# Expert blocks of a hybrid convolution/attention kernel: the first layer's products regrouped from pairs to triples

## The chip, the cores and the metric

The kernel runs on one core of one Trainium2 chip, in fp32 throughout. The metric is the time of one execution in device microseconds, as the median of repeated runs. The engines named below are TensorE (PE, its weight loads PEld), VectorE (DVE), ScalarE (ACT), GpSimd (POOL) and the DMA-issuing SyncE (SP).

## The reference, cut to what matters

The program computes a grid layer with sampled attention, a window attention and, last, a mixture of four experts over 4096 tokens of 384 channels. The change touches the experts:

```python
scores = jnp.einsum('bsd,de->bse', x, gate_w) + gate_b       # 4 experts
probs = jax.nn.softmax(scores, axis=-1)                      # the two best are kept and normalised
h = jax.nn.gelu(jnp.einsum('bsd,edh->ebsh', x, w1) + b1[:, None, None, :], approximate=False)
y = jnp.einsum('ebsh,ehd->ebsd', h, w2) + b2[:, None, None, :]
out = jnp.einsum('bse,ebsd->bsd', masked, y)                 # x: 384 channels, h: 1536, y: 384
```

Each token goes through two of the four experts. For one expert, the first layer is a product of the tokens (384 channels) with a 384 x 1536 matrix, followed by a bias and a GELU; the second layer is a product with a 1536 x 384 matrix.

## The kernel before, in words

The first 1690 us or so of the execution are the grid layer, the window attention and the router; they were placed by a planner and by the framework's scheduler. The change touches them at two places: the number of buffers of the `kv` tile in `keys` (line 2356), and the loop in `outputs` (line 2447) that hands POOL one weight sum per token tile for the first expert block.

The experts are 25 blocks in a fixed order (`ORDER`, line 43): blocks 0 to 12 hold 512 rows, 13 to 15 hold 256, 16 to 24 hold 128. Blocks 1, 2 and 12 follow a 512-row block directly; 3, 5, 7, 9, 10 and 11 stand behind a 128-row block, 4, 6 and 8 behind a 256-row one. Inside this stage the instructions of all five engines stand in the order in which the program writes them (a manual schedule), and every engine works its queue in order.

A block takes its rows by an indirect DMA a block ahead (`gather`), its weights by SP (`first_weights`, `second_weights`), turns the rows on PE into channels on partitions (`turn`: four transposes into a PSUM tile and one copy to `xT`, for each of three channel groups), and then runs the two layers.

For 512 and 256 rows (`long_block`) the first layer saves multiplications. The hidden units come in 12 groups of 128, taken as six pairs; the tokens come in two halves of `m` = 256 (or 128) columns. Channel groups 0 and 1, two hidden groups and two token halves form a 2 x 2 by 2 x 2 block product that is done with seven products P1 to P7 (a Winograd form) in place of eight; channel group 2 is multiplied plainly (`plain`). The class `Pair` holds the steps: `alpha` (P1, P5 and a copy of P1 by ACT), `beta` (P2, P3), `gamma` (P6, accumulated over P1 in the left half of the PSUM tile `y`), `after_gamma` (a second copy, then two DVE additions), `delta`, `after_delta`, `epsilon`, and `gelu`. The sums of weights that the products need are made by POOL (`first_sums_steps`: four additions per half of the weights, so eight per block), the sums of token halves by DVE (`token_sums`: four additions).

The second layer is always the seven-product form (`second_product`, six products of 192 columns for each token tile), with weight sums on POOL (`second_sums`) and sums of the hidden values on DVE (`hidden_sums`). `add_rows`, `add_bias` and `store_rows` add the weighted results to the output rows that `rows_so_far` has read, and POOL stores them by indirect DMA. A block of 128 rows (`short_block`) uses plain products in both layers.

While block j runs, its `hooks("start")` puts on POOL's queue the second half of its own weight sums, the second layer's sums, the reading of the output rows, and the first half of the next block's weight sums; `hooks("between")` issues the weights and the gather for block j + 2. The next block's rows are turned, and its token sums made, inside the second layer of the present one.

PSUM tiles come from three pools: `ltr` (2 buffers, transposes), `lmm` (4 buffers: the pairs' `x` and `y`, and some accumulators) and `lph` (2 buffers). SBUF scratch of the first layer is `snap` and `third`, two buffers each.

## Time and profile before

| what | us |
|---|---|
| median of 15 runs | 2721.13 (2711.2 to 2728.9) |
| the profiled execution's own time | 2719.35 |
| its span in the trace | 2717.7 |
| PE busy | 2517.0 (93%) |
| DVE busy | 1801.6 (66%) |
| POOL busy | 1357.3 (50%) |
| ACT busy | 1102.8 (41%) |
| PE busy in the stretch 1800 to 2000 us (experts) | 197.93 of 200 |
| ACT, DVE, POOL busy in that stretch | 47.90, 89.28, 90.18 |

The experts' stage runs from about 1691 us (the first transposes of block 0) to the end. One line of the profile stands for one instruction or for a run of equal ones; an fp32 product of PE is two instructions, so "x2" in a line of PE is one product. A line gives the start, the duration, the engine, the line of the kernel, the operation, the tile written and those read, their shapes, and in brackets how long the engine had been idle and what ended that.

### The profile page before, as it was taken

What the parts mean: (1) busy time and instruction counts of PE and PEld (TensorE: products, weight loads), DVE (VectorE), ACT (ScalarE), POOL (GpSimd) and SP (SyncE); (2) the same over time, 40 slices, a digit from 0 to 9 for tenths busy, and PEclk for the clock granted to TensorE, in tenths of its full rate; (3) what the DMA queues carried; (4) which work ended last, traced back from release to release, by engine and by line L of the source; (5) the groups of instructions that cost most, each with busy time, mean ns of one, the idle gap of its engine ahead of it and who ended that gap; (6) DMA issues with size and microseconds to landing.
All of it is one profiled execution on the core that took longest, in us unless ns stands there. A gap on an engine that the chain in (4) does not pass through costs nothing. (4 is left out here: it accounts for less than half of the span.)

```text
span 2717.7 us, 39372 instructions
## 1 busy us (share of the span) xinstructions
PE 2517.0 (93%) x15017; PEld 1590.4 (59%) x15017; DVE 1801.6 (66%) x2921; ACT 1102.8 (41%) x1818; POOL 1357.3 (50%) x1132
## 2 busy tenths in 40 slices
PE   8877976899999999999999997899999999999999
PEld 5434533333333333333366664788878888888888
DVE  3655856998999999999957666644354454434443
ACT  5543542565666666666533331222232222122222
POOL 1334845665566556666401255444384454544453
PEclk9877977999999999999999998899999999999999
DMA  7554437555555665555221313235455545544441
GB/s 212 150 142 133 127 103 208 168 161 173 146 156 169 192 177 165 161 153 160 81 93 47 120 59 104 87 121 170 150 190 184 179 146 183 184 164 158 164 144 36
DMA packets 263321, 395.44 MB, mean 146 GB/s; under 512 B 134674, under 2 KB 207634, under 8 KB 262748
## 3 DMA queue, kind: packets, MB, share of 16 engines
q1 hardware_dynamic: 214912, 230.43, 27.5%
q0 software_dynamic: 47504, 162.42, 19.5%
q8 instruction: 119, 1.95, 0.3%
q14 instruction: 70, 0.57, 0.1%
q10 hardware_dynamic: 716, 0.07, 0.0%
HBM read 335.95 MB, written 70.06 MB: 149 GB/s over the span
## 5 line engine op out<-in xcount | busy, mean ns | idle before, releaser
L1443 PE MATMUL ps<-q,k 64*64 64x512 f32 (+1 forms) x1632 | 380.4, 583 | 33.5 <-DVE S L1475 16.9
L1448 PE MATMUL ps<-t,o 64*64 64x512 f32 (+3 forms) x1536 | 351.8, 572 | 0.0
L1324 POOL DMA_INDIRECT win<-table,widx x192 | 283.5, 1477 | 69.5 <-issue 24.7
L1015 POOL DMA_INDIRECT ga<-img,pidx x168 | 192.0, 1143 | 234.1 <-DVE w L972 70.1
L2564 POOL DMA_INDIRECT out<-rows,ei x67 | 67.3, 1004 | 415.2 <-DVE rows L2557 394.0
L1475 DVE SCALAR_TENSOR_TENSOR S<-t,bw,ps 128x1024 f32<-128x1024 f32 x192 | 237.1, 1277 | 32.0 <-PE ps L1448 29.5
L1385 ACT ACTIVATE t<-win,bw 128x1056 f32<-128x1056 f32 x192 | 207.4, 1092 | 120.0 <-DVE S L1475 99.4
L1443 PEld LDWEIGHTS ps<-q,k 64*64 64x64 f32 x1632 | 103.9, 134 | 251.8 <-issue 187.0
L1548 POOL TENSOR_TENSOR S<-S,pbs 128x896 f32<-128x896 f32 (+1 forms) x69 | 136.7, 1982 | 203.2 <-DVE t L1396 197.5
L1553 ACT ACTIVATE S<-S 128x2048 f32<-128x2048 f32 x96 | 183.4, 1911 | 96.9 <-DVE S L1540 88.8
L1567 PE MATMUL po<-S,v 128*64 128x512 f32 x768 | 191.5, 610 | 24.0 <-ACT S L1553 23.5
L1396 DVE SCALAR_TENSOR_TENSOR t<-win,bw,t 128x1056 f32<-128x1056 f32 (+3 forms) x169 | 196.1, 1196 | 12.6 <-ACT t L1385 12.5
L2661 PE MATMUL b<-w,h 128*128 128x192 f32 x1044 | 180.3, 326 | 0.0
L856 PE MATMUL pcv<-qpad,wc 64*64 64x256 f32 x1728 | 144.0, 414 | 34.7 <-issue 32.5
L2661 PEld LDWEIGHTS b<-w,h 128*128 128x128 f32 x1044 | 171.3, 190 | 2.4
L1540 DVE TENSOR_TENSOR S<-S,pbs 128x2048 f32<-128x2048 f32 (+1 forms) x96 | 158.9, 1657 | 12.4 <-ACT pbs L1529 12.4
L2493 DVE COPY d_xT<-e_tr 128x512 f32<-128x512 f32 (+2 forms) x75 | 37.6, 511 | 172.4 <-PE e_tr L2490 152.3
L2600 ACT COPY snap<-y 128x256 f32<-128x256 f32 (+1 forms) x96 | 33.8, 352 | 271.0 <-PE y L2583 263.2
L2257 POOL DMA_INDIRECT tab_d<-ent,si x64 | 65.9, 1030 | 146.2 <-DVE selw L2250 126.4
L2615 DVE TENSOR_TENSOR snap<-y,snap 128x256 f32<-128x256 f32 (+1 forms) x96 | 38.3, 399 | 151.1 <-ACT snap L2614 136.7
L2757 ACT ACTIVATE h<-ph,b1c 128x128 f32<-128x128 f32 x108 | 30.8, 368 | 265.1 <-PE ph L2751 265.1
L856 PEld LDWEIGHTS pcv<-qpad,wc 64*64 64x64 f32 x1728 | 83.4, 145 | 89.1 <-issue 69.7
(413 smaller groups left out, 5745.3 us busy)
## 6 DMA issues: line engine op xcount, KB each, us to landing
w<-in_L_ffn_w SPq DMA_DIRECT2D x50, 2304.0 KB
img<-in_x SPq DMA_DIRECT2D x48, 256.0 KB
q<-q_d SPq DMA_DIRECT2D x48, 256.0 KB
x<-in_x SPq DMA_DIRECT2D x8, 768.0 KB
q_d<-qt SPq DMA_DIRECT2D x24, 256.0 KB
v_d<-qkvw SPq DMA_DIRECT2D x32, 192.0 KB
k<-k_d SPq DMA_DIRECT2D x48, 128.0 KB
v<-v_d SPq DMA_DIRECT2D x24, 256.0 KB
```

What stands on the lines that cost most here:

```text
L856: nc.tensor.matmul(ps[s][h * GC : (h + 1) * GC, :], wc[half, t, c, :], qpad[half, c, y0 : y0 + 8, dx : dx + WI], start=(t == 0), stop=(t = ...
L1015: nc.gpsimd.indirect_dma_start(out=ga[:, g].rearrange("p s c -> p (s c)"), out_offset=None, in_=img[b][:, :], in_offset=bass.IndirectOffse ...
L1324: i_ = nc.gpsimd.indirect_dma_start(out=win[:, : (WROWS - free_rows(nb)) * WIN], out_offset=None, in_=tables[h // 2][:, :], in_offset=bass ...
L1385: i_ = nc.scalar.activation(t.rearrange("p y x -> p (y x)"), wins[p, e][:, :n], AF.Copy, scale=weight(p, e, 0),)
L1396: state["gate"] = nc.vector.scalar_tensor_tensor(tf, wins.pop((p, e))[:, WIN : WIN + ts[p, e].shape[1] * WIN], weight(p, e, 1), tf, ALU.mu ...
L1443: made.append(nc.tensor.matmul(ps[HALF[1 - r], e, q_at], k[HALF[r], 2 * kp + e, :], q[HALF[r], q_at], start=(step == 0), stop=(step == 1 a ...
L1448: made.append(nc.tensor.matmul(ps[HALF[r], d, at], os_[p, d][HALF[r], :], wholes[p, d][HALF[r], at.start // WI : at.stop // WI, 0:WI], sta ...
L1475: nc.vector.scalar_tensor_tensor(st[:, e, :].rearrange("p (y x) -> p y x", x=WI), wholes.pop((p, e))[:, :, 1:WIN], weight(p, e, 3), ps[:, ...
L1540: state["gate"] = nc.vector.tensor_tensor(at_, at_, bc(pbss[p // KP][:, cols_], 1, 2), ALU.add)
L1553: nc.scalar.activation(Ss[p], Ss[p], AF.Exp)
L1567: nc.tensor.matmul(pos[i][0][HALF[f], :], vs[i][:, 2 * kp + e, :], Ss[p][:, e, FULL[f]], start=(first and e == 0), stop=(last and e == 1),)
L2661: nc.tensor.matmul(out[:, k * NH : (k + 1) * NH], h[:, v, k * P : (k + 1) * P], w[:, v, :], start=(start and v == 0 and k == 0), stop=True ...
```

## The change

Blocks of 512 rows get another first layer; blocks of 256 rows keep the pairs (now in a function `by_pairs`, with the same steps); blocks of 128 rows keep plain products. For 512 rows the hidden groups are taken as four triples, and all three channel groups, three hidden groups and two token halves form a 3 x 3 by 3 x 2 block product that is done with 15 products q1 to q15 in place of 18. The class `Trio` holds its steps. Six products (`alpha(0)` to `alpha(5)`) accumulate one after the other in the right half of the PSUM tile `x`, and ACT copies the running sum to SBUF after each of the first five; five products (`beta(0)` to `beta(4)`) accumulate in the right half of the PSUM tile `y`, and DVE adds the running sum to a copy after each. `shared`, `one`, `two` and `three` are the other four products.

`by_threes` interleaves the first five alphas of the next group with the present group's other products by a written string of letters: `A` is an alpha of the group ahead, `a5` the present group's sixth alpha, `b` a beta of the present group, `q`, `r`, `s` and `p` are `shared`, `two`, `three` and `one`, `w` a beta of the group before, `v`, `z` and `u` GELUs, `f` a product of the second layer that fills the last group. The first five alphas of a block's first group are issued by `begin` inside the block before.

POOL now makes 13 weight sums of 256 columns per half of the weights (26 per block), DVE 12 sums of token halves in two parts and ACT one negated copy; the copies of the transposes to `xT` move from DVE to ACT; the transposes and the token sums stand at earlier places in the second layer of the block before; P1 and P2 of the second layer are split to wait for the last GELUs. In the router stage, POOL is handed up to four sums per token tile, and `kv` has two buffers in place of three. The scratch `xc` has one buffer of ten parts in place of two of three; `th`, `tg` and `tc` have two each.

```diff
-                kv = c2.tile([P, 2 * NC], F32, tag="kv", bufs=3, name=f"kv{b}_{k}")
+                kv = c2.tile([P, 2 * NC], F32, tag="kv", bufs=2, name=f"kv{b}_{k}")
...
-                i_ = next(sums, None)
-                if i_ is not None:
+                for i_ in itertools.islice(sums, 4):
                     then(i_, y_)
...
+        t = flat.rearrange("p (k g j) -> p k g j", k=6, j=P)
+        n0, n1, n2, n3, n4, n5 = (t[:, k] for k in range(6))
+        d["A", half] = dict(
+            q1=a31, q2=a11, q3=n5, q4=n2, q5=a12, q6=n3, q7=n4, q8=a13, q9=n1, q10=n0, q11=a21, q12=a23, q13=a22,
+            q14=a32, q15=a33,
+        )
+        for out_, one, other, op in (
+            (n0, a21, a33, ALU.add), (a31, a31, a32, ALU.add), (n1, a21, a31, ALU.add), (a31, a11, a31, ALU.add),
+            (n2, a32, a31, ALU.subtract), (n2, n2, a33, ALU.subtract), (n3, a13, a23, ALU.subtract),
+            (n4, a21, n3, ALU.subtract), (n3, n3, a22, ALU.add), (n5, a31, a12, ALU.add), (n5, n5, n3, ALU.subtract),
+            (a23, a23, a33, ALU.add), (a23, a23, a22, ALU.subtract),
+        ):
+            yield nc.gpsimd.tensor_tensor(out_, one, other, op)
...
-            nc.vector.tensor_copy(d["xT"][:, c, :n], pt[:, :n])
+            nc.scalar.copy(d["xT"][:, c, :n], pt[:, :n])
...
+            if part == 0:
+                nc.scalar.mul(x9, b11, -1.0)
+            for out_, one, other, op in (
+                (
+                    (x0_, b12, b11, ALU.subtract), (b12, b12, b22, ALU.subtract), (x1, b12, b32, ALU.subtract),
+                    (x2, b11, x1, ALU.subtract), (x3, b11, b22, ALU.subtract),
+                ),
+                (
+                    (x6, b32, b31, ALU.subtract), (x7, x6, b12, ALU.subtract), (x5, b21, b31, ALU.add),
+                    (x4, b21, b22, ALU.subtract), (b21, b11, b21, ALU.subtract), (x8, b22, b31, ALU.add),
+                    (b32, b22, b32, ALU.add),
+                ),
+            )[part]:
+                nc.vector.tensor_tensor(out_, one, other, op)
...
+        class Trio:
...
+            def alpha(self, k):
+                if k == 0:
+                    self.x = lmm.tile([P, 512], F32, tag="mm", name="x")
+                    self.th = dh.tile([P, 512], F32, tag="th", bufs=2, name="th")
+                    self.tg = dh.tile([P, 512], F32, tag="tg", bufs=2, name="tg")
+                    self.tc = dh.tile([P, 256], F32, tag="tc", bufs=2, name="tc")
+                self.product(("q10", "q11", "q9", "q1", "q2", "q4")[k], self.x, self.right, start=k == 0)
+                if k < 5:
+                    to = (
+                        self.th[:, self.right], self.th[:, self.left], self.tc[:, : self.m], self.tg[:, self.left],
+                        self.tg[:, self.right],
+                    )[k]
+                    nc.scalar.copy(to, self.x[:, self.right])
+
+            def beta(self, k):
+                if k == 0:
+                    self.y = lmm.tile([P, 512], F32, tag="mm", name="y")
+                self.product(("q15", "q12", "q6", "q8", "q7")[k], self.y, self.right, start=k == 0)
+                if k < 4:
+                    to = (
+                        self.tc[:, : self.m], self.th[:, self.left], self.tg[:, self.left], self.tg[:, self.right]
+                    )[k]
+                    nc.vector.tensor_tensor(to, self.y[:, self.right], to, ALU.add)
+                else:
+                    nc.vector.tensor_tensor(self.y[:, self.both], self.y[:, self.both], self.th[:, self.both], ALU.add)
+
+            def shared(self):
+                self.z = lph.tile([P, 512], F32, tag="ph", name="z")
+                self.product("q3", self.z, self.left, start=True)
+                to = self.tg[:, self.right]
+                nc.vector.tensor_tensor(to, self.z[:, self.left], to, ALU.add)
+
+            def one(self):
+                self.product("q5", self.z, self.left)
+                to = self.tg[:, self.left]
+                nc.vector.tensor_tensor(to, self.z[:, self.left], to, ALU.add)
+
+            def two(self):
+                self.product("q13", self.y, self.left)
+
+            def three(self):
+                self.product("q14", self.x, self.left)
+                to = self.x[:, self.left]
+                nc.vector.tensor_tensor(to, to, self.tc[:, : self.m], ALU.add)
...
+        def begin(d):
+
+            if d is None or short(d) or middle(d):
+                return
+            d["first"] = t = Trio(d, 0)
+            for k in range(5):
+                t.alpha(k)
+                yield
...
+            for g in range(last + 1):
+                was, t, ahead = t, ahead, Trio(d, g + 1) if g < last else None
...
+                for what in (
+                    "A0 v a5 w4 A1 z q b0 A2 r b1 A3 s b2 A4 u p b3" if g < last else
+                    "f v a5 w4 f z q b0 f r b1 f s b2 f u p b3 f f f b4 x"
+                ).split():
...
+                    elif what == "q":
+                        t.shared()
+                    elif what == "r":
+                        t.two()
+                    elif what == "s":
+                        t.three()
+                    elif what == "p":
+                        t.one()
...
+                    elif was and what[0] == "w":
+                        was.beta(k)
...
+            if nxt:
+                token_sums(nxt, 0)
             second_product(d, "P7", b1_, range(HV), False)
...
+            third, more = second_steps(d, "P3", b3_, range(HV), False), begin(nxt)
+            for _ in third:
+                next(third, None)
+                next(more, None)
+            for _ in more:
+                pass
...
+            if nxt:
+                token_sums(nxt, 1)
             add_rows(d, low, 1, b3_)
             store_rows(d, low)
```

## The prediction

> **What bounds the kernel now.** The page's slices come first: in the experts' stage (from 1691 us) PE stands at 9 nearly throughout. Then one 512-row block, cut at its last first-layer products, in the table by stretches.
>
> ```profile
> PE   8877976899999999999999997899999999999999
> ```
>
> ```profile
> core 0: us, PE busy (x) PEld busy (x) DVE busy (x) ACT busy (x) POOL busy (x), PEclk, DMA share, GB/s
> 1771.40:1800.10 28.70, 28.55 (x124) 22.70 (x123) 9.65 (x19) 13.30 (x28) 25.85 (x21) 1.00 0.44 143
> 1800.10:1828.90 28.80, 28.80 (x181) 28.56 (x180) 17.54 (x30) 1.53 (x3) 1.48 (x2) 1.00 0.26 93
> ```
>
> PE is filled in both layers at granted clock 1.00; DVE and ACT have room, POOL is full in the first half and idle in the second. So PE's products, and waits that interrupt them, set the time. The groups by shape give the prices of the steps between products.
>
> ```profile
> L2616 DVE TENSOR_TENSOR x<-x,snap 128x512 f32<-128x512 f32 x78 | 54.6, 700 | 8.3 <-DVE snap L2615 0.5
> L2615 DVE TENSOR_TENSOR snap<-y,snap 128x256 f32<-128x256 f32 x78 | 33.1, 424 | 134.4 <-ACT snap L2614 120.0 <-issue 14.3
> L2600 ACT COPY snap<-y 128x256 f32<-128x256 f32 x78 | 29.0, 372 | 242.8 <-PE y L2583 237.7 <-remote 3.9 <-ACT third L2631 1.0
> L2122 POOL TENSOR_TENSOR wa<-w 128x384 f32<-128x384 f32 x30 | 30.5, 1015 | 2.5 <-PE y L2590 2.2
> L2523 POOL TENSOR_TENSOR wb<-w 128x1152 f32<-128x1152 f32 x15 | 39.4, 2627 | 0.0
> ```
>
> Last, the timeline of the one place in a 512-row block where PE waits today, for the delays between engines.
>
> ```profile
> 1773.99 0.59 PE L2583 MATMUL y<-xc,wa 128*128 128x256 f32 x2
> ...
> 1774.63 0.37 ACT L2614 COPY snap<-y 128x256 f32<-128x256 f32 x1 [0.86 <-issue]
> ...
> 1774.86 0.59 PE L2583 MATMUL x<-d_xT,wa 128*128 128x256 f32 x2
> ...
> 1775.03 0.42 DVE L2615 TENSOR_TENSOR snap<-y,snap 128x256 f32<-128x256 f32 x1 [2.68 <-ACT snap L2614]
> 1775.56 0.70 DVE L2616 TENSOR_TENSOR x<-x,snap 128x512 f32<-128x512 f32 x1
> 1775.57 0.30 PEld L2583 LDWEIGHTS y<-d_xT,w 128*128 128x128 f32 x2 [0.52 <-issue]
> 1775.60 0.67 PE L2583 MATMUL y<-d_xT,w 128*128 128x256 f32 x2
> ...
> 1776.11 0.59 PE L2590 MATMUL y<-d_xT,w 128*128 128x256 f32 x2
> ...
> 1776.34 0.69 ACT L2620 ACTIVATE h<-x,b1c 128x512 f32<-128x512 f32 x1 [1.34 <-DVE x L2616]
> ```
>
> The reader is to see: products follow each other by 0.431 us. A reader of PSUM starts 0.63 after its product's start (1773.99, 1774.63). The stalled product counts as begun at 1775.68 (the next comes 0.43 later), so 0.23 after the DVE addition's end (1775.45); after an ACT copy the weight load follows by 0.05, hence 0.16. ACT starts 0.08 after a DVE addition (1776.26, 1776.34). And P7, which writes the left half of `y`, waits for L2615, which reads the right half: a PSUM tile is waited for whole.
>
> **Products (a gain).** A pair has nine products of 256 columns and one of 512: 6 x 11 = 66 steps of 0.431. The triples have 4 x 15 = 60. 6 x 0.431 = 2.59 us saved per block. The stall shown (1775.68 for 1775.29: 0.39) goes too. Together -2.98.
>
> **Wait 1: `th` (the chain is not three apart here).** alpha(0) of the group ahead is copied into `th`, which has two buffers; that buffer is the one of the group before, and is free only when beta(4)'s 512-column addition has read it. The built instruction order lists this wait on ACT's copy, in the second and third triple of each block. But beta(4) (`w4`) is issued after A0, one product before A1, which needs the copy. From the start of w4: addition from 0.63 to 1.33, copy from 1.41 to 1.78, A1 at 1.94 in place of 0.43: 1.51 lost. Behind the waiting copy stand two GELUs (0.69 each, needed a group later) and A1's copy; the second GELU ends 0.2 before A2's copy is due, so nothing more is lost. 2 x 1.51 = 3.02 per block.
>
> **Wait 2: `two`.** q13 goes to the left of `y`, whose right half the addition of beta(0) is reading; the built order shows the wait, as for P7 above. From b0: the addition runs 0.63 to 1.05, r counts at 1.28; its place is 0.86. 0.42, in four groups (0.52 in the last, where a 0.326 us filler stands for an alpha): 1.78 per block. The other betas are three products apart, 1.29 against 1.28: covered, by nothing to spare; in the last group 1.19, 0.09 late three times: 0.27.
>
> **Starting a block.** An alpha with its copy turns round in 0.63 + 0.37 + 0.16 = 1.16. Between two second-layer products (0.65) it comes every 1.08: four times 0.08, and 0.30 at A1, where only a5 lies between: 0.62.
>
> Sum per 512-row block: -2.98 + 3.02 + 1.78 + 0.27 + 0.62 = **+2.71**. For the 12 blocks after block 0: +32.5. Block 0 alone has its five alphas bare (4 x 0.73), before its gain; the start before had stalls of its own (1.2 to 3 us in PE's waits); I take 0, between -3 and +8.
>
> **Weight and token sums (POOL, DVE).** A 256-column addition is estimated at 0.75 on the line through 1.015 and 2.627, with the 0.05 between dependent ones about 0.79: 13 take 10.3 where four took 4.3. Between 512-row blocks POOL's idle second half holds them. Behind a 128-row block there is no such room:
>
> ```profile
> 1887.54 0.98 POOL L2564 DMA_INDIRECT out<-rows,ei  x1 [0.31 <-issue]
> 1894.87 0.99 POOL L2536 DMA_INDIRECT rows<-out,ei  x1 [6.34 <-DMA out<-rows,ei]
> ```
>
> ```profile
> 1898.28 1.10 DVE L2505 TENSOR_TENSOR xc<-d_xT,xc 128x256 f32<-128x256 f32 x1
> ```
>
> POOL waits for a store to land, then reads rows and sums from R = 1894.87. The token addition that takes 0.42 elsewhere takes 1.10 beside POOL's sums: DVE lets POOL's addition end first. In the changed order, DVE's bias addition waits for the rows (1902.55 before, R + 7.7), 0.6, then come the seven sums of part 1, five beside POOL at 0.8 each until R + 12, two more at full speed, a row addition (0.6), the addition of `shared` and that of b0, done at R + 14.5, so r counts at R + 14.7. PE reaches the block 2.5 later than before (five alphas and their stalls; 1902.45 + 2.5 = R + 10.1), A0, a5, A1 (0.30 late), q, b0, A2 take it to R + 13.0, and wait 2 would let r go at R + 13.2: **1.5 late**, between 0 (DVE not slowed) and 3.5 (three more waits of 0.7). Six such blocks: 9.0. Block 11 has four gathers ahead of its second half's sums, not one (3 x 1.27): 1.5, between 0 and 4. Behind the three 256-row blocks only three alphas have products between them (two bare, 0.65 more each), and the first waits about 1 for token sums; those blocks' own 2 us wait (P6 on DVE's rows, below) shrinks: +2 each, between -1 and +4: 6.
>
> ```profile
> PE b L2661 <- DVE rows L2557: 5.4, 3, 2.1
> ```
>
> **Elsewhere.** The 26 early sums end before POOL's next work (idle 31 us until 1639.62); two `kv` buffers suffice, since PE issues the product that frees one before the matmuls that refill it. Bounds 0 to +5 (the wait of PE's `pa` for `kv` is 3.3 in all). ACT gains three copies of about 0.6 and one negation per block where it is idle (1.53 busy of 28.8): hidden; without cover, 0.6 each.
>
> **Clock.** The 2.06 us wait above is followed by a granted clock of 0.59 over 2002 to 2006; waits of 1.23 and 1.27 near 1711 and 1715 are not, nor is one of 1.7 between 2260 and 2400 (1.00 over 2200 to 2400). At 1.51 I take 0, up to +10.
>
> The Trainium skill's "TensorE: Matmul & The Clock Gate", section "Why this matters for your kernels", asks only for no idle gap over some 3 us. By it not even the 2.06 us gap would have mattered, and the term and its upper bound would be 0; here the row decides.
>
> **Sum.** 32.5 + 0 + 9.0 + 1.5 + 6 = 49.0 on the profiled execution's own 2719.35: 2768. That execution lies 1.8 below the median of 15, so 2770.
>
> **Rivals.**
> Late sums hidden: DVE and POOL lose nothing behind short blocks, only the waits inside the block stay: 2721 + 33 = 2754. With 0.16 instead of 0.23 for DVE's way back to PE (the copy's; six times 0.07 in each of 13 blocks, 5 in all) and the low bounds of start and 256-row blocks, 2743. For it: DVE was idle 10 us before those sums. Against: 1.10 for 0.42.
> Sums and clock at their upper bounds: 49 + 6 x 2 + 2.5 + 3 x 2 = 69.5, so 2790, and up to 2813 with clock, start and `kv`; half-way in, 2783 on. For it: 2002 to 2006.
> The other side: the two waits overlap work. If DVE served beta(4) and beta(0) so that waits 1 and 2 together cost under 2.1 of their 4.8 per block, the blocks would gain; with both at 0, 12 x -2.1 = -25, and -8 with the sums: 2696 to 2713. The waits stand in the built order, so only the prices could be wrong, by half.
> The announced spacing is itself a rival that fails: were all links three apart, wait 1 would be 0.
>
> **How the numbers follow.** Likeliest, 0.52: 2758 to 2783. Late sums hidden 0.22, upper bounds 0.19, other side 0.05, no change 0.02. Leaving out the far ends of the rivals gives 2745 to 2798. Within 0.2% (5 us, what can be told from no change): 0.02; faster 0.05; slower 0.93.
>
> **What would show it.** In the changed profile: twice per 512-row block a PE gap near 1.5 us at A1, released by an ACT copy to `th` that itself waited for a 512-column DVE addition; a gap of 0.4 before q13 in each triple, released by DVE; 512-row blocks 2.7 us longer, 57.5 to 60.2; gaps of 1 to 2 us in the first triple behind 128-row blocks. I am wrong if PE runs A0, a5, w4, A1 at 0.43 steps.

## The result and the profile after

The changed kernel takes 2768.02 us (median of 9 runs, 2753.8 to 2778.51) where the kernel before takes 2721.86 (46 runs): 1.0166 times as long, 95% interval 1.0150 to 1.0182. The forecast was 2770. The profiled execution took 2764.45 with a span of 2762.7, 45.0 more than the span before. So the total agrees; the terms it was made of agree less well, and this is the more useful reading.

PE's waits in the experts, longest in total first (total, times, longest), from the waits of the changed kernel from 1690 us on:

```profile
PE x L2694 <- ACT th L2711: 38.4, 27, 6.4
PE y L2694 <- DVE tc L2721: 12.1, 19, 2.1
...
PE y L2631 <- DVE snap L2663: 2.7, 5, 1.3
...
PE x L2694 <- POOL wa L2150: 1.8, 1, 1.8
```

The first line is wait 1 of the prediction (A1's product waits for ACT's copy to `th`), 24 of 27 in pairs in the blocks behind block 0. The second is wait 2 (q13 waits for DVE's addition of the first beta) and, in its longest cases, the late token sums. The waits of P6 for DVE's rows, 5.4 us before, don't occur in this profile (in a second profile of the changed kernel they are 2.6), and for POOL's first-layer sums there is one wait of any size, in block 11.

Wait 1 and wait 2 in block 1, on the timelines of PE, DVE and ACT (start, duration, what; in brackets the idle time and its end):

```profile
1789.01 0.59 PE L2694 MATMUL x<-xc,wa 128*128 128x256 f32 x2
1789.44 0.59 PE L2694 MATMUL x<-d_xT,wa 128*128 128x256 f32 x2
1789.87 0.59 PE L2694 MATMUL y<-d_xT,wa 128*128 128x256 f32 x2
1791.72 0.70 PE L2694 MATMUL x<-xc,w 128*128 128x256 f32 x2 [1.25 <-ACT th L2711]
1792.26 0.59 PE L2694 MATMUL z<-d_xT,wa 128*128 128x256 f32 x2
1792.69 0.59 PE L2694 MATMUL y<-xc,w 128*128 128x256 f32 x2
1793.12 0.59 PE L2694 MATMUL x<-xc,wa 128*128 128x256 f32 x2
1793.80 0.70 PE L2694 MATMUL y<-xc,w 128*128 128x256 f32 x2
1794.34 0.59 PE L2694 MATMUL y<-d_xT,w 128*128 128x256 f32 x2
```

```profile
1790.51 0.70 DVE L2723 TENSOR_TENSOR y<-y,th 128x512 f32<-128x512 f32 x1 [0.87 <-PE y L2694]
...
1793.32 0.42 DVE L2721 TENSOR_TENSOR tc<-y,tc 128x256 f32<-128x256 f32 x1
```

```profile
1791.29 0.37 ACT L2711 COPY th<-x 128x256 f32<-128x256 f32 x1 [1.99 <-DVE y L2723]
```

These are A0, a5, w4 at steps of 0.43, then A1 at 1.85 behind w4, where 0.43 would do: w4's product, DVE's addition of 512 columns (ends 1791.21), ACT's copy (1791.29 to 1791.66), A1 at 1791.72. The product behind A1 comes at 0.54, not 0.43. So the wait costs 1.42 + 0.11 = 1.53; the prediction had 1.51. q13 at 1793.80 comes 0.68 behind A2, with 0.54 behind it: 0.25 + 0.11 = 0.36, where the prediction had 0.42. The addition that it waits for ends at 1793.74.

Behind a 128-row block (block 3), DVE, PE and POOL:

```profile
1916.30 0.84 DVE L2597 SCALAR_TENSOR_TENSOR rows<-b2r,en,rows 128x384 f32<-128x384 f32 x1 [4.84 <-DMA rows<-out,ei]
1917.07 0.95 DVE L2556 TENSOR_TENSOR xc<-d_xT 128x256 f32<-128x256 f32 x1
1918.05 0.83 DVE L2556 TENSOR_TENSOR xc<-xc,d_xT 128x256 f32<-128x256 f32 x1
...
1921.40 0.41 DVE L2556 TENSOR_TENSOR xc<-d_xT 128x256 f32<-128x256 f32 x1
...
1922.93 0.41 DVE L2721 TENSOR_TENSOR tc<-y,tc 128x256 f32<-128x256 f32 x1
```

```profile
1920.70 0.59 PE L2694 MATMUL x<-xc,wa 128*128 128x256 f32 x2
1923.40 0.70 PE L2694 MATMUL y<-xc,w 128*128 128x256 f32 x2 [2.10 <-DVE tc L2721]
```

```profile
1909.23 0.99 POOL L2584 DMA_INDIRECT rows<-out,ei  x1 [7.55 <-DMA out<-rows,ei]
```

With R = 1909.23 the rows let DVE go at R + 7.1 (forecast R + 7.7), the additions take 0.83 to 0.95 beside POOL's sums and 0.41 when those are done, b0's addition ends at R + 14.1 and q13 starts at R + 14.2 (forecast R + 14.7).

What each stretch of the experts takes, from the first transposes of a block to those of the block behind it (differences of starts on PE's timeline; "+" joins blocks):

| stretch | before | changed | difference |
|---|---|---|---|
| block 0 | 67.21 | 69.13 | +1.9 |
| block 1; block 2 | 57.47; 57.46 | 59.87; 59.87 | +2.4 each |
| 16+3, 18+5, 20+7, 22+9, 23+10 | 73.58, 73.58, 73.58, 73.78, 73.58 | 78.08, 77.81, 77.26, 76.56, 77.75 | +4.5, +4.2, +3.7, +2.8, +4.2 |
| 24+11 | 73.57 | 79.66 | +6.1 |
| 17+13+4, 19+14+6, 21+15+8 | 110.31, 108.30, 108.36 | 110.23, 109.99, 110.84 | -0.1, +1.7, +2.5 |
| block 12 to the end | 75.69 | 81.98 | +6.3 |

In a 512-row block the changed kernel transposes the next rows 12 second-layer products, 3.9 us, earlier (behind P4, not behind P6): so block 0 is really 5.8 longer and block 12 is 2.4 longer. The start of the stage lies 2.5 later than before. These differences add up to the 45.0.

### The profile page after: what moved, and what is told of

Read it like the earlier page. It is cut to its first block, busy times and chain, and to the rows that moved or that the text cites. A ratio compares the mean times of both kernels' runs of the same rounds, so it can differ in the third digit from the quotient of the medians.

```text
span 2762.7 us, 39983 instructions
## 1 busy us (share of the span) xinstructions
PE 2504.6 (91%) x15017; PEld 1574.3 (57%) x15017; DVE 1884.9 (68%) x3132; ACT 1141.4 (41%) x1932; POOL 1525.5 (55%) x1366
## 5 line engine op out<-in xcount | busy, mean ns | idle before, releaser
L2783 PE MATMUL b<-w,h 128*128 128x192 f32 x1044 | 188.7, 326 | 0.0
L857 PE MATMUL pcv<-qpad,wc 64*64 64x256 f32 x1728 | 136.5, 409 | 36.7 <-issue 34.8
L2605 DVE SCALAR_TENSOR_TENSOR rows<-b,en,rows 128x192 f32<-128x192 f32 x232 | 85.3, 411 | 121.0 <-PE b L2783 95.6
L2694 PE MATMUL x<-xc,w 128*128 128x256 f32 x312 | 101.2, 406 | 42.3 <-ACT th L2711 38.4
L2517 ACT COPY d_xT<-e_tr 128x512 f32<-128x512 f32 (+2 forms) x75 | 32.8, 453 | 220.0 <-PE e_tr L2514 220.0
L2150 POOL TENSOR_TENSOR wa<-w 128x256 f32<-128x256 f32 x130 | 109.4, 842 | 16.5 <-PE y L2694 12.4
```

The source lines that it names most:

```text
L857: nc.tensor.matmul(ps[s][h * GC : (h + 1) * GC, :], wc[half, t, c, :], qpad[half, c, y0 : y0 + 8, dx : dx + WI], start=(t == 0), stop=(t = ...
L2783: nc.tensor.matmul(out[:, k * NH : (k + 1) * NH], h[:, v, k * P : (k + 1) * P], w[:, v, :], start=(start and v == 0 and k == 0), stop=True ...
```

## The experiments

The runs fell on chips of two kinds. On those with the numbers 14, 1 and 10 the kernel before takes 2634 to 2636 us, on number 11 it takes 2723. For the first profiles of both kernels no number is on record; by their time (2722) they belong with number 11. Where an expectation speaks of the second or the other chip, the kind is meant. The experts' blocks take the same time on both kinds (999.9 and 999.8 us in the last column for the changed kernel), block 0 excepted. Every ratio is against the kernel before, run beside it. The last column is the time from block 1's first transposes to the end, in one profile; the kernel before has 959.3 and 957.5 in two profiles, and 3.9 has to be added to these for a comparison, because its transposes stand 3.9 later. The rows with "+" build on "all three", each on the one with "+" above it; a later place for the gather replaces the earlier one.

| kernel | median | before | ratio (95%) | blocks 1 to 12 and their short ones |
|---|---|---|---|---|
| changed | 2768.02 | 2721.86 | 1.0166 (1.0150 to 1.0182) | 999.9 |
| changed, faster kind of chip | 2677.36 | 2633.71 | 1.0168 (1.0151 to 1.0185) | 999.8 |
| third `th` | 2636.34 | 2636.06 | 1.0002 (0.9990 to 1.0013) | 964.9 |
| q13 by b0 | 2657.27 | 2636.06 | 1.0082 (1.0065 to 1.0099) | 985.7 |
| bias later | 2669.51 | 2636.06 | 1.0123 (1.0104 to 1.0141) | 995.7 |
| all three | 2615.07 | 2636.06 | 0.9919 (0.9902 to 0.9936) | 943.3 |
| + late gather | 2617.67 | 2633.71 | 0.9938 (0.9921 to 0.9954) | 947.5 |
| + wider start | 2611.97 | 2633.71 | 0.9925 (0.9909 to 0.9942) | 944.2 |
| copies on DVE | 2681.01 | 2633.71 | 1.0178 (1.0161 to 1.0195) | 1007.4 |
| + gather behind all sums | 2703.90 | 2722.65 | 0.9935 (0.9913 to 0.9957) | 944.4 |
| + rows first | 2700.10 | 2722.65 | 0.9921 (0.9891 to 0.9951) | 941.8 |
| + early gather | 2602.15 | 2635.67 | 0.9877 (0.9854 to 0.9899) | 930.5 |

**Wait 1 taken away.**

```diff
-                    self.th = dh.tile([P, 512], F32, tag="th", bufs=2, name="th")
+                    self.th = dh.tile([P, 512], F32, tag="th", bufs=3, name="th")
```

> The changed kernel with three buffers for th in place of two, nothing else. Theory (wait 1 of the prediction): in the changed profile A1 starts 1.85 us after the product before it, where 0.43 would do, and the product after it follows at 0.54 where 0.43 would do, so the wait costs 1.53; it stands twice in each of 13 blocks, 40 us. With a third buffer the copy of group g+1 has nothing to wait for: 2768 - 40 = 2728 us, between 2722 and 2736, and the waits of x for th fall from 38.4 us to under 8 (block 0 has one of 6.4 that DVE's own standstill makes). Rival: the waits only show that DVE and ACT set the pace, and the time comes back at the next link of a chain (q13 or a beta waiting for DVE): 2755 to 2768, with the waits of y for tc risen from 12 us to 30 or more.

The changed kernel's 1.0168 on a kernel before of 2636.06 is 2680; this one has 2636.34, 44 less. Blocks 1 and 2 take 56.81 and 56.82, 3.06 and 3.05 less than 59.87, two waits of 1.53. PE's waits:

```profile
PE y L2694 <- DVE tc L2721: 14.2, 21, 2.8
...
PE x L2694 <- ACT th L2711: 1.0, 2, 0.6
```

The time did not come back at q13: the first line was 12.1 and is 14.2. The rival, that DVE and ACT set the pace, falls. One buffer of 2 KB a partition is the whole difference between a loss of 1.7% and none.

**Wait 2 taken away.**

```diff
                 self.product(("q15", "q12", "q6", "q8", "q7")[k], self.y, self.right, start=k == 0)
+                if k == 0:
+                    self.product("q13", self.y, self.left)
...
-                    "A0 v a5 w4 A1 z q b0 A2 r b1 A3 s b2 A4 u p b3" if g < last else
-                    "f v a5 w4 f z q b0 f r b1 f s b2 f u p b3 f f f b4 x"
+                    "A0 v a5 w4 A1 z b0 A2 q b1 A3 s b2 A4 u p b3" if g < last else
+                    "f v a5 w4 f z b0 f q b1 f s b2 f u p b3 f f f b4 x"
```

> The changed kernel with q13 issued directly after the first beta's product and ahead of DVE's addition to it, and the string otherwise the same with q moved to where r stood; th keeps two buffers. Theory (wait 2): q13 starts 0.25 late in three groups of a block and 0.36 in the last, each with 0.11 more at the product after it, 1.55 us per block; all go, and the next beta stands three products behind: 13 x 1.55 = 20, so 2748 us, between 2742 and 2756; wait 1 stays as it is (38 us of x waiting for th). Rival: the addition comes one product later, because DVE now has to wait for q13 too, and the next beta waits in q13's place: 2762 to 2768.

2657.27, some 23 under the 2680 where 20 were expected. Blocks 1 and 2 take 58.55 and 58.80, 1.1 to 1.3 less, not quite 1.55: in block 1 three other products come 0.05 to 0.10 late that didn't before. PE's waits:

```profile
PE x L2694 <- ACT th L2711: 33.4, 27, 1.4
...
PE y L2694 <- DVE tc L2723: 3.5, 6, 0.9
```

b0 and q13 now run as one pair (1.03 for four instructions at 1704.71) with the next beta three products behind; wait 1 is untouched, as it should be. The second line was 12.1: part of the late sums behind short blocks is covered too, since the first reader of DVE's addition now stands later.

**Late sums.**

```diff
-            add_bias(d, 0)
             if nxt:
                 token_sums(nxt, 1)
+            add_bias(d, 0)
             second_layer(2, True)
```

> The changed kernel with the bias addition of a 128-row block moved on DVE's queue from ahead of the second part of the next block's token sums to behind it; nothing else. Theory (late sums, as the prediction worked them out): DVE stands still for 4.8 us at the bias addition because the rows have not landed, and the seven sums begin only at R + 7.7; moved ahead of it they begin when their input is there, R + 2.3, run slowed beside POOL until about R + 9, and the first q13 behind a 128-row block loses its extra wait, 2.1, 1.8, 1.3, 0.6, 1.8 and 1.6 at blocks 3, 5, 7, 9, 10 and 11, 9 us in all: 2759 us, between 2755 and 2764. Rival: the sums are late because they are slowed beside POOL's sums, not because of the rows; then the gain is under 3: 2765 to 2770.

2669.51, 11 under the 2680; the interval of the difference is some 5 either way. In the profile the last column falls by only 4.1, less than half of what was expected. The pairs 16+3, 18+5, 20+7, 22+9 and 23+10 take 76.29, 76.06, 76.05, 76.06 and 76.05, the 73.6 of before plus 2.4, so their late sums are gone. DVE's timeline behind block 16 in this kernel:

```profile
1824.41 0.83 DVE L2556 TENSOR_TENSOR xc<-xc,d_xT 128x256 f32<-128x256 f32 x1
...
1828.63 0.94 DVE L2556 TENSOR_TENSOR d_xT<-d_xT 128x256 f32<-128x256 f32 x1
1829.49 1.08 DVE L2597 SCALAR_TENSOR_TENSOR rows<-b2r,en,rows 128x384 f32<-128x384 f32 x1
```

The sums are as slow beside POOL as ever, 0.83 to 0.94, yet end at 1829.6, in time. Standing behind an addition that waits for rows is what made them late; the slowing alone doesn't, and the rival falls. What the slowing adds while they stand there was not tried alone. But 24+11 takes 81.41, 2.3 more than in the changed kernel on this kind of chip (79.13), because PE now comes sooner and meets POOL:

```profile
2552.50 0.70 PE L2694 MATMUL x<-xc,wa 128*128 128x256 f32 x2 [2.75 <-POOL wa L2150]
...
2556.66 1.06 PE L2694 MATMUL z<-d_xT,wa 128*128 128x256 f32 x2
2557.52 1.06 PE L2694 MATMUL y<-xc,w 128*128 128x256 f32 x2
```

Behind the wait the products come 0.85 apart, not 0.43: over 2554 to 2560 the granted clock is 0.50, which costs some 2.3 us more (from A0 at 2552.50 to A3 it is 8.20 where the steps of the changed profile make 5.87). The run with q13 by b0 has the same: a wait of 2.50 for `wa`, half the clock behind it, and 81.23 for 24+11. DVE's lateness had covered a part of POOL's: of the 9 us expected, the 1.6 of block 11 turned into another wait and a slower clock behind it.

**All three.**

> The three edits together: third buffer for th, q13 beside the first beta, bias addition behind the token sums. Theory: the three waits lie at different places of PE's queue and their gains add: 2768 - 40 - 20 - 9 = 2699 us, between 2690 and 2712, which is less than the kernel before. What stays over the 15-product blocks' own saving is the slow start (0.7 a block) and block 0's standstill (5). Rival: DVE and ACT set the pace once the first wait is gone, and the gains overlap: 2715 to 2740.

2615.07, 65 under the 2680 and 21 under the kernel before. In the traces the gains add: 34.9, 14.1 and 4.1 of the single edits make 53.1 of the last column's time, and together they save 56.5. Blocks 1 and 2 take 55.51 and 55.50; inside block 1, behind A1 of the first triple, no first-layer product comes more than 0.1 late.

**The changed kernel on the faster kind of chip.**

> The changed kernel itself, beside the kernel before, on the chip of the following runs: the runs with a third th buffer and so on lay on a chip where the kernel before took 2636 us, not 2722. Theory: the experts' blocks take the same time there (57.47 us for a block of 512 rows behind another in the kernel before, 59.87 in the changed one), so the difference of 46 us stays as it is in us: before + 42 to + 48. It may be under the 45 by up to 6, since the standstill of 6.4 us in block 0 of the first profile is absent from the four profiles of the second chip. Rival: the difference belonged to the chip and scales with the early stages.

+43.7, and blocks 1 and 2 take 59.86: the loss in us is the same and doesn't scale with the early stages (the stage starts at 1616, not at 1694). Block 0 takes 61.07, not 69.13.

**Late gather.** Behind a 128-row block the gather of the block after next moves from ahead of the present block's second half of sums to behind it.

```diff
                             first_sums(d, 1)
+                            if "late" in d:
+                                d["late"]()
                             second_sums(d, 0)
...
-                        gather(ds[j + 2], homes[j % 2][1])
+                        if short(d):
+                            nxt["late"] = lambda e=ds[j + 2], at=homes[j % 2][1]: gather(e, at)
+                        else:
+                            gather(ds[j + 2], homes[j % 2][1])
```

> The kernel with all three edits, and besides, behind a 128-row block the gather of the block after next is issued behind the present block's second half of weight sums on POOL, not ahead of them. Theory (block 11's term): four gathers of 1.27 us and a conversion stand ahead of block 11's second half of sums; in the profile with all three edits PE waits 2.6 us for a wa of POOL and the stretch from block 24's transposes to block 12's is 76.3 us where the same stretch at blocks 9 and 10 is 71.7 and 72.1, so 4 us are to be had there and 0 to 0.5 at each of the other eight blocks behind a short one: 3 to 6 us under the kernel with all three edits, which stood 21 us under the kernel before: before - 24 to before - 27. Rival: the sums of the second half are late for another reason (POOL's wait for the rows to be stored): no more than 1 us gained.

A miss: 16 under the kernel before, where the three edits had 21 and 24 to 27 were expected. 24+11 fell from 76.27 to 71.69, as worked out, but the same queue now has the gather ahead of the 256-row blocks' second-layer sums and of block 11's reading of rows:

```profile
PE b L2785 <- POOL wb L2575: 7.3, 3, 2.7
...
PE b L2785 <- DVE rows L2605: 2.1, 1, 2.1
```

The two waits of 2.75 for `wb` (at 2089.90 and 2271.69) are followed by half the clock for some 3 us, and these two 256-row stretches take 109.15 and 109.24; behind the third wait, of 1.80, the clock stays whole, and that stretch takes 106.71. I had counted what the moved instructions were freed from, and not all that they were put in front of.

**Wider start.** Behind 512 rows the five first alphas stand three second-layer products apart.

```diff
-            second_product(d, "P7", b1_, range(HV), False)
-            third, more = second_steps(d, "P3", b3_, range(HV), False), begin(nxt)
-            for _ in third:
-                next(third, None)
-                next(more, None)
+            more = begin(nxt)
+            third = itertools.chain(
+                second_steps(d, "P7", b1_, range(HV), False), second_steps(d, "P3", b3_, range(HV), False)
+            )
+            for k, _ in enumerate(third):
+                if k in ((10, 13, 16, 19, 22) if q == 2 else (5, 7, 9, 10, 11)):
+                    next(more, None)
...
-                    if beside:
+                    if hc in (6, 7, 8, 10, 11):
```

> The kernel with the late gather, and besides, the five first alphas of a block spread over more of the second layer before it: behind a 512-row block three products apart in place of two, behind a 256-row block from two products earlier on, behind a 128-row block from two products earlier on with two products between the third and the fourth. Theory (start of a block, 0.71 a block in the changed profile: 0.41 between the alphas and 0.30 at A1): behind 512 rows 0.4 goes, three times; behind 128 rows 0.3, six times; behind 256 rows, where two bare alphas cost 0.7 each, about 1, three times: 6 us in all, so before - 30 to before - 33. Rival: the alphas, earlier, wait for token or weight sums that are not ready, above all behind 128-row blocks: 0, or slower by up to 6.

Blocks 1 and 2 take 55.11 and 55.10, 0.40 less, as the 0.41 between the alphas says. Behind 128-row blocks 0.2 to 0.7 goes. Behind the 256-row blocks nothing comes of it (107.04, 109.28, 109.04 against 106.71, 109.15, 109.24): the alphas, earlier, wait for `xc`, and POOL's late `wb` stays. The last column shrinks by 3.3, half of what was expected; the median is 21.7 under the kernel before, where 30 to 33 were expected.

**Copies back on DVE,** in the changed kernel.

```diff
-            nc.scalar.copy(d["xT"][:, c, :n], pt[:, :n])
+            nc.vector.tensor_copy(d["xT"][:, c, :n], pt[:, :n])
```

> The changed kernel with the copies of the transposes back on DVE, one part of the change undone. Theory (the prediction cost the move to ACT at nothing, since ACT is idle there): behind 512-row blocks DVE is idle too (2 to 4 us between row additions), so nothing changes there; behind 128-row blocks DVE gets three copies of 0.7 at 512 columns, or 0.4 where the rows are fewer, ahead of the token sums, which are not the last to come there (DVE waits for the rows), so 0 to 6 us: between the changed kernel - 2 and + 6. Rival: the move is what took away the 1.8 us waits of the kernel before behind P6 in the three 256-row blocks, which the prediction missed; then undoing it costs 5 to 10 us, and PE's waits of b for rows of DVE stand again at 5 us.

The medians can't tell the two (1.0178 against 1.0168); the traces can, with one profile of each: the three 256-row stretches take 113.51, 111.97 and 112.62 against 110.25, 110.73 and 110.89, 6.2 in all, and block 0 takes 2.1 more. Blocks 1 and 2 stay at 59.86. The waits:

```profile
PE x L2694 <- DVE xc L2556: 4.0, 3, 1.3
...
PE b L2783 <- DVE rows L2605: 3.7, 6, 1.0
```

So the move to ACT is worth 6 us where 256-row blocks end. It is between the theory and its rival. The wait of P6 for rows is 3.7 without the move and 2.6 with it, so the rival's 5 us are not there. But the first alpha's wait for token sums, which the prediction took for certain (1 us each), is there only with the copies on DVE.

**The kernel before, once more.**

> The kernel before, for a profile on the chip of the other runs. Open is block 0: the first profiles have 67.21 us from its transposes to block 1's in the kernel before and 69.13 in the changed one (whose transposes stand four of P's products later, 3.9 us), but 61.07 in the changed kernel's profile of the second chip. Theory: the standstills of block 0 (PE 3.0 us 'issue' in the kernel before; DVE 4.8 us 'remote' in the changed one) and the half clock behind them belong to the execution, not to the code; then the kernel before has 57 to 61 here. Rival: the kernel before has 67 again, and the changed kernel gains 6 in block 0 on this chip. Both ways the other blocks take what they took in the first profile: 57.47 for blocks 1 and 2, 73.6 for a pair of a 128-row and a 512-row block.

This run fell on chip 11, of the first profiles' kind, so it doesn't settle block 0 on the faster kind. It took 67.36 there, as before. The stretch 17+13+4 took 108.59, not 110.31: the wait of 2.06 us in the first profile is 1.47 here, and the granted clock behind it is 1.00, not 0.59.

**Two places for the gather, and one for the rows.** First behind all of the second layer's sums, and only where the block holds 512 rows; then besides, in 256-row blocks, DVE's addition of P1's results ahead of the hidden sums.

```diff
-                            if "late" in d:
-                                d["late"]()
                             second_sums(d, 0)
                             rows_so_far(d)
                             second_sums(d, 1)
+                            if "late" in d:
+                                d["late"]()
...
-                        if short(d):
+                        if short(d) and not middle(nxt):
                             nxt["late"] = lambda e=ds[j + 2], at=homes[j % 2][1]: gather(e, at)
...
+            if middle(d):
+                add_rows(d, low, 0, b1_)
             hidden_sums(d, 0)
             hidden_sums(d, 1)
-            add_rows(d, low, 0, b1_)
+            if not middle(d):
+                add_rows(d, low, 0, b1_)
```

> All edits so far, with the late gather only where the block behind the 128-row block holds 512 rows, and placed behind the second layer's sums and the reading of the rows. Theory: in the profile with the wider start PE waited 2.7 us in each of the three 256-row blocks for wb of POOL (four gathers had moved ahead of these sums) and 1.8 us for rows of DVE in block 11's second layer (the rows were read five us later); both go, 10 us less: before - 30 to before - 34. Rival: the sums of these blocks are late in any place (DVE and POOL slow each other there), and under 4 us are gained: before - 22 to before - 26.

> As the kernel ahead of it in this list, and in the 256-row blocks DVE adds P1's results to the rows ahead of the first two sums of hidden values, not behind them. Theory: P6 waits about 0.97 us in each of these blocks for that addition, because DVE's first sum of hidden values takes 3.3 us beside POOL's sums; moved ahead, the addition is done while P2 and P4 run, and what stays is P6's wait for the sum itself: 0 to 3 us less than the kernel ahead of it, which five rounds can hardly tell apart; the waits of b for rows of DVE are the reading (2.6 us before, 0 after). Rival: the addition now waits for P1 and holds up the sums behind it on DVE; P6 waits for the sums, as long or longer.

The first is a miss again, 18.8 under the kernel before, where 30 to 34 were expected. The three 256-row stretches came down to 105.54, 105.47 and 106.16, 8 less as expected, but block 12 rose from 79.26 to 85.67: its rows now come after it wants them, and behind the waits the granted clock is 0.66 over 2622 to 2632.

```profile
PE e_tr L2514 <- DMA xr<-tn_d,ei: 5.6, 4, 1.9
```

The second can't be told from the first, in medians or stretches (105.87, 105.02, 105.96). There was nothing to win: with the gather moved, PE no longer waits for rows of DVE in these blocks in either kernel.

**Early gather.** POOL stands 6 to 7 us at the start of each 128-row block until a store has landed; the gather goes there, and the load of its entries goes ahead of the weights on SP.

```diff
+                        if j and j + 2 < N_BLK:
+                            ds[j + 2] = tokens_of(j + 2, ds0)
                         if nxt:
                             second_weights(nxt, *homes[(j + 1) % 2])
-                        if j and j + 2 < N_BLK:
-                            ds[j + 2] = tokens_of(j + 2, ds0)
...
+                            if short(d) and j + 2 < N_BLK:
+                                gather(ds[j + 2], homes[j % 2][1])
                             first_sums(d, 1)
...
-                            if "late" in d:
-                                d["late"]()
...
-                        if short(d) and not middle(nxt):
-                            nxt["late"] = lambda e=ds[j + 2], at=homes[j % 2][1]: gather(e, at)
-                        else:
+                        if not short(d):
                             gather(ds[j + 2], homes[j % 2][1])
```

> As the kernel with the rows first, but the gather that was put late (behind all sums) is put early: at the start of a 128-row block, ahead of POOL's reading of the output rows, where POOL stands still for 6 to 7 us until a store has landed; and SP issues the load of the entries (en) that the gather needs ahead of the 2304 KB of second-layer weights, not behind them. Theory: in the profile of the kernel with the late gather the transposes of block 12 waited 5.6 us for their rows, and the stretch from them to the end took 84 to 86 us where it takes 77.6 with the gather at its old place; block 11's stretch keeps its 71.6 (76.3 at the old place). Both together, block 12 near 77.2 and block 11 near 71.6: 7 us less than the kernel with the rows first, so before - 27 to before - 31. Rival: en comes late, POOL stands longer and the weight sums behind it come late in all nine blocks behind a short one: before - 10 to before - 20, with waits of x for wa of POOL.

2602.15, 33.5 under the kernel before, somewhat more than the 27 to 31 expected: 0.9877, interval 0.9854 to 0.9899, the shortest of all. 24+11 takes 71.53 and block 12 77.23. The two moves, on POOL's queue and on SP's, weren't tried apart. All waits of PE in the experts for ACT, DVE and POOL that are left (those for `pg` and `e_tr` and the start of block 0 aside) are short:

```profile
PE x L2694 <- DVE xc L2556: 1.6, 3, 0.8
PE x L2694 <- ACT th L2711: 1.5, 3, 0.6
PE y L2631 <- DVE snap L2663: 1.5, 3, 0.8
```

A 512-row block takes 55.10 against the 57.47 of before. The smaller first layer is worth 2.4 a block once its chains wait for next to nothing; 0.26 at A1 of the first triple stays.

## Why the prediction was right, step by step

The sign, the mechanism and the size of the largest terms are shown by the runs. That the sum of 49.0 comes so near to the 45.0 in the profile is in part luck: the 512-row blocks came out 3.7 smaller than forecast and the 256-row stretches 9.1 smaller, while block 0 came out 5.8 larger, the start of the stage 2.5 and the late sums 0.5.

| term | predicted | measured | by |
|---|---|---|---|
| products and gamma, per block | -2.98 | -2.9, what is left of the +2.40 without the three waits of 3.06, 1.55 and 0.71 | subtraction |
| wait 1, per block | +3.02 | +3.06 | third `th` |
| wait 2, per block | +1.78 | +1.55 in the trace, +1.1 to 1.3 when removed | q13 by b0 |
| last group's betas, per block | +0.27 | under 0.1 | timeline |
| start, per block | +0.62 | +0.71 | timeline, wider start |
| a 512-row block behind another | +2.71 | +2.40 | stretches |
| late sums, behind six 128-row blocks, with block 11 | +10.5 | +11.0 | stretches |
| three 256-row stretches beyond the 512-row block in them | +6 | -3.1 in the first profiles of both kernels, -0.5 in the second ones | stretches |
| block 0 | 0 | +5.8 on the slower kind of chip | stretches |
| `kv` and early sums | 0 | between -0.1 and +1.5 | router to stage's start |

**Wait 1** stands at A1 in each block twice, is released by the copy to `th`, which waited for the 512-column addition, and goes with a third buffer.

**Wait 2** was mis-sized: the prediction charged 0.23 for the way from DVE back to PE. q13 starts 0.06 behind the end of the addition, and the restart costs 0.11 more at the next product, 0.17 in all. The rows show the same for ACT's copy (1791.66 to 1791.72, then 0.54).

**Late sums** agree in size and moment (q13 at R + 14.2 for R + 14.7). Of the cause, the place behind the bias addition that waits for rows is shown, by moving it; how much the slowing beside POOL adds there is not. What the prediction had not worked out is that this lateness covered a part of block 11's wait for its gathers: 1.8 us of it stands in the changed profile, 2.75 where the lateness is taken away.

**256-row blocks** were the term that failed. The prediction charged two bare alphas and a wait for token sums, +2 a block, and granted little for the 2 us wait that would shrink. In the first profile of the changed kernel that wait is not there at all (0.9 a block in the second), and the alphas find their token sums ready; that this is what won back the cost of the bare alphas is likely, but the two were not tried apart. One of the three stretches of before also held a half clock that the second profile of before does not have: against that profile the term is 1.64 + 1.64 + 2.57 - 7.2 = -1.4, and -0.5 with the second profile of the changed kernel too (1.66 + 2.38 + 2.62 - 7.2). The copies on ACT, which the prediction cost at nothing, are worth 6 here.

**Block 0** was put at 0, between -3 and +8. Its five bare alphas were charged 4 x 0.73 on top of their places. In both profiles of the changed kernel they stand 1.68 apart, at a granted clock of 0.50 (over 1700 to 1713 in the first), so they cost 4 x 1.25, 2.1 us more:

```profile
1706.50 1.22 PE L2694 MATMUL x<-xc,w 128*128 128x256 f32 x2 [0.46 <-ACT th L2711]
1708.19 1.22 PE L2694 MATMUL x<-xc,wa 128*128 128x256 f32 x2 [0.46 <-DVE r_row L2337]
```

The kernel before has 0.50 over 1698 to 1709 as well, so the price at full clock was the wrong one for this place. Besides, the first alpha stands 11.1 us behind the first transposes where the first product of before stood 9.7 behind them. On the slower kind of chip DVE then stands still at w4's addition:

```profile
1728.68 0.70 DVE L2723 TENSOR_TENSOR y<-y,th 128x512 f32<-128x512 f32 x1 [4.81 <-remote]
```

```profile
1722.78 0.70 PE L2694 MATMUL y<-d_xT,wa 128*128 128x256 f32 x2 [1.48 <-issue]
1729.90 1.22 PE L2694 MATMUL x<-xc,w 128*128 128x256 f32 x2 [6.42 <-ACT th L2711]
```

The product that the addition needs ended by 1723.5; wait 1's chain turns the standstill into 6.42 us for PE. All five profiles on the slower kind of chip have such a "remote" stop of DVE or ACT that ends between 1721 and 1730, also the two of before; the nine on the faster kind have none, and the changed kernel's block 0 takes 61.07 there. The expectation that the stop belongs to the execution is therefore wrong: it belongs to the kind of chip, or to the moment at which its stage starts. What causes it is open, and so is what the change does to block 0 on the faster kind, where the kernel before has no profile.

**The early stages.** The stage starts 2.5 later than before, but 1.1 of that is there when the router begins (its first `c_kv` at 1381.2, not 1380.1), and the two profiles of before differ by 1.3. From that `c_kv` to the stage it is 311.1 and 311.6 us in the profiles of before, 312.5 and 311.5 in those of the changed kernel. The two `kv` buffers and the early sums weren't tried alone.

**Clock.** It was put at 0, and the 1.25 us gaps leave the granted clock at 1.00, over 1780 to 1800 and over 1840 to 1860, each with such gaps. The 6.42 us gap of block 0 is followed by 0.54 over 1729 to 1735. The rule of the Trainium skill that the prediction set against its row ("TensorE: Matmul & The Clock Gate", section "Why this matters for your kernels") agrees with both of these. It does not with the 2.06 us gap of before, with 0.59 behind it, nor with the experiments: of the eleven waits of PE between 2.50 and 2.77 us in their experts' blocks behind block 0, seven are followed by half the clock for about 3 to 7 us, four are not (2.77 at 2443.49 with the third `th`). So the row was the better guide. That the term came out at 0 owes something to luck: the changed kernel has waits of 2.10 in the first profile and 2.53 in the second, and behind both the clock stayed at 1.00.

**DVE beside POOL.** The Trainium skill's "SBUF — State Buffer", section "Who interferes with whom", says that a DVE instruction with two inputs in SBUF contends with a GpSimd instruction that reads SBUF, and that one with at most one such input, outside the 2-port perf modes, doesn't. The trace agrees: token additions (two inputs in SBUF) take 0.83 to 0.95 beside POOL's sums and 0.41 without, while additions with one input in PSUM take 0.42 beside them (1925.86, with POOL adding from 1924.36 to 1931). The prediction had DVE let POOL's addition end first, as if DVE alone lost; POOL's additions at 1916.81 and 1917.69, beside these, take 0.92 and 0.91 where the six ahead of them take 0.72 to 0.73.

## What to carry to other kernels

An interleaving that keeps dependent links three products apart has to be read for tiles, not only for values: the two losses here were a scratch buffer that came round one group too early and the other half of a PSUM tile that an addition was still reading, and both show in the built order before anything runs. Price such a wait from the chain product, addition, copy, product, and give the scratch as many buffers as there are groups in flight (three here: the group before, still to be read, the present one and the one ahead). A wait of over 2 us on PE can cost nearly as much again in granted clock (2.3 us behind one of 2.75 here). When instructions are moved on an in-order queue, count everything that they are put in front of; the free place is where the queue already stands still for something else.

## What was not expected of the hardware

The way from DVE or ACT back to a waiting PE is 0.06 us, and the product behind the restarted one starts 0.54 behind it instead of 0.43: 0.17 in all, where 0.23 had been read for DVE from the kernel before. DVE and ACT stop for 2 to 6 us in block 0 in all five profiles on the slower kind of chip and in none of the nine on the faster. Half the clock stood behind seven of eleven PE waits of 2.50 to 2.77 us, and no run shows what decides it. Beside POOL's sums the four DVE additions of 768 columns in one 256-row block took 2.27, 1.36, 1.15 and 1.15 us (from 2013.74 on), the first of them 3.29 in another profile, while POOL's own sums of 256 columns went from 0.72 to 1.50: which of the two loses, and how much, changes from one instruction to the next.
